# Pools that lie over released ones: waits tile by tile instead of for the whole pool, in a two-layer graph network on one core

## The chip, the core and the metric

The kernel runs on one core of a Trainium2 chip. Its engines are named as the profile names them: PE (matrix products), DVE, ACT and POOL (element-wise work; POOL also issues indirect transfers), and SP, which only issues transfers. Each engine works through its own instructions in order. The metric is the device time of one execution in microseconds (us), as the median of several runs.

## The reference: what is computed

The input is 64 graphs of 256 nodes with 256 features (16384 rows in all) and an integer adjacency. Two layers, each with a graph part and a feed-forward part, all with a residual and a layer norm ahead:

```python
x = x + attention(norm(x), adj, W, a)            # layer 0, graph: softmax over neighbours
x = x + mamba2(norm(x), W_in, conv_w, ..., b_lin) # layer 0, feed-forward: a scan over each graph
x = x + relational(norm(x), adj, weight, bias)   # layer 1, graph
x = x + moe(norm(x), gate_w, gate_b, w1, b1, w2, b2)  # layer 1, feed-forward
```

The last one matters here. Each row is given to the one of 8 experts with the highest gate value, at most 2560 rows to an expert:

```python
idx = argmax(softmax(x @ gate_w + gate_b)); pos = running count of rows of that expert
buf[idx, pos] = x                                  # rows beyond the capacity are dropped
hmid = relu(buf @ w1[e] + b1[e]);  ybuf = hmid @ w2[e] + b2[e]
y = ybuf[idx, pos] * probability * kept
```

## The kernel before: two passes, and the memory they share

**Preparation.** `first_pass` opens a pool `wts` for what lasts through pass 1 and, inside it, the pools `prep` and `prep_ps` (L514 on), in which weights are folded together. The last product there is a transpose of the expert biases b1 (L588); DVE copies it out (L590) and SP writes it to a DRAM tensor `b1d` (L591). Then `prep` and `prep_ps` are released, and their bytes in SBUF and their PSUM banks become free for others.

**Pass 1** works on 32 groups of two graphs (512 rows). Its tiles come from one pool, `fast_pool`, and eight PSUM banks, `fast_ps`; both lie over the released `prep` pools. `clear_slots` fills a DRAM table `slots` with a far value through a tile `blank` (L615 on POOL, L616 a transfer on ACT's queue). For each group SP loads x (L803) and adj (L805); PE transposes x (L781) and so on through attention, scan and relational part. At the end of each pair of groups `choose` picks the experts, and POOL scatters one 4-number record for each row into `slots` (L1282). The order in which all five engines receive their instructions in pass 1 is written out by a planner (`Plan`) from fixed costs and due times (PACE, DUE, LATE); it is the same before and after the change.

When all rows are chosen, `list_blocks` makes on DVE the lists of work for pass 2 (L635 to L647, into the tile `work`). Beside this the plan runs two blocks of 512 rows of the expert part early, in the bytes of pass 1's own tiles (`first_block`: products L744 and L1388, row arithmetic on DVE L1394, L420 to L424, L1402 and on ACT L1396, and an indirect scatter of the finished rows to the output, L427 on POOL). The `y` tiles of these blocks have four buffers, so a later row tile is written over an earlier one whose scatter must have landed.

**Pass 2** (`second_pass`) does the rest of the expert part. Its pools `et`, `es` and `eps` lie over pass 1's released ones. A block is 128, 256 or 512 rows of one expert: kinds "quarters", "halves" and "wholes". Ahead of the loops stands a prologue for all three kinds, in this order: slot fetches of blocks 0 and 1 of each kind (SP, L1502, six transfers, each after reading the list with L1494); index copies and gathers of their rows (POOL, L405, L406, L409: 14 gathers of 128 rows, 2 + 4 + 8); the first weights of each kind (SP, w1 L1511, b1 L1514, w2 L1517, b2 L1520; w1 and w2 are 1 MB each); row norm (DVE L415), transposes (PE L1545) and their copies (ACT L1548) of block 0 of each kind. Then, under nested conditions on the counted number of blocks (L1593, L1619), the quarters run, then the halves, then the wholes. A block i asks for the weights of i+1 and the slots and rows of i+2, computes its hidden layer (PE L1563, ACT L1567) and its output (PE L1573, DVE L1578, ACT L1579, DVE row arithmetic), and scatters (L427). Weights have two buffers, slots and rows three. SP and POOL take all this in the order of the program.

A second version of both passes ("slow", for adjacency values that the fast one does not cover) stands behind a condition and does not run with these inputs.

Of the kernel before, what the change touches and what calls it, by code (L numbers as in the profile page):

```python
# [16 lines left out]
PSUM = bass.MemoryType.PSUM  # L17
# [270 lines left out]
def gnn_mamba_rgcn_moe(ctx: ExitStack, tc: tile.TileContext, a: dict, out: bass.AP):  # L288
# [143 lines left out]
    def first_pass(form, pass1):  # L432
# [73 lines left out]
        def relation(pool, banks, dst, r):  # L506

            nc.sync.dma_start(
                out=dst[:, :, 0:D], in_=a["L1_gnn_weight"][r].rearrange("(k p) o -> p k o", p=P)
            )  # L510
            centred(pool, banks, dst[:, :, 0:D], dst[:, :, 0:D], D)
            projected(pool, banks, dst[:, :, D:DG], dst[:, :, 0:D], E + 1)

        with tc.tile_pool(name="prep" + form, bufs=1) as prep, tc.tile_pool(  # L514
            name="prep_ps" + form, bufs=2, space=PSUM
# [96 lines left out]
        def clear_slots(pool):  # L612

            blank = pool.tile([P, E * CAPP * 4 // P], F32, tag="wh", name="blank", bufs=1)
            nc.gpsimd.memset(blank, FAR)  # L615
            nc.scalar.dma_start(out=slots.rearrange("(p j) w -> p (j w)", p=P), in_=blank)  # L616
            nc.vector.memset(seen, 0.0)
# [33 lines left out]
        def list_first(s):  # L651


            v = nc.vector
            tot, full, ends, gap = (s.tile(n + "_", [P, E]) for n in ("tot", "full", "ends", "gap"))
            we, wb, past = (s.tile(n + "_", [P, NEARLY]) for n in ("we", "wb", "past"))
            counted(s, tot)

            def filled():
                v.tensor_scalar(full(), tot(), 512.0, None, ALU.is_ge)  # L660
                for i in range(2, NB + 1):
                    v.scalar_tensor_tensor(full(), tot(), 512.0 * i, full(), ALU.is_ge, ALU.add)

            s.step(DVE, 0.5, filled, [tot], [full])

            def ended():
                v.tensor_copy(ends(), full())
                summed_up(ends())

            s.step(DVE, 0.8, ended, [full], [ends])  # L670

            def took():
                v.tensor_scalar(tot(), ends(), float(NEARLY), None, ALU.min)
                v.tensor_copy(taken[:, 0:1], tot()[:, 0:1])
                v.tensor_sub(taken[:, 1:], tot()[:, 1:], tot()[:, : E - 1])
                v.tensor_scalar(gap(), full(), -1.0, float(NB), ALU.mult, ALU.add)
                v.tensor_copy(wb(), num[:, :NEARLY])

            s.step(DVE, 0.5, took, [ends, full], [tot, gap, wb, s.fixed(taken)])
            walk(s, we, wb, past, NEARLY, ends, gap, NBLK, early)  # L680
# [726 lines left out]
        def group(s, g, js, pair, toks, full=False):  # L1407


            s.of(g)  # L1410
            xe, hide, entries = attention(s, g, js, full)
            ahead = scan(s, g, xe)
            adjT = mix(s, xe, entries, full, *ahead)
            relate(s, js, 4 * (g % 2), full, xe, adjT, pair)
            if g % 2:
                s.of(g + 1, first=False)
                choose(s, toks, pair)
# [3 lines left out]
            mybir.EngineType.Pool, mybir.EngineType.SP,  # L1421
        }
        if form == "fast":
            pool = pass1.enter_context(tc.tile_pool(name="fast_pool", bufs=1))
            banks = pass1.enter_context(tc.tile_pool(name="fast_ps", bufs=1, space=PSUM))
            clear_slots(pool)
            plan = Plan(pool, banks)

            GEARLY = NG - 4
            rows_early = plan.fixed(x3d)  # L1430
            for g in range(NG):
                if g % 2 == 0:
                    pair = {"stored": [rows_early] if g < GEARLY else []}
                group(plan, g, slice(4 * g, 4 * g + 4), pair, tok[:, 4 * (g - 1) : 4 * (g + 1)])
                if g == GEARLY - 1:
                    plan.after(NG)
                    list_first(plan)
            plan.after(NG)
            list_blocks(plan)
            for b in range(NEARLY):  # L1440
                first_block(plan, b, rows_early, x3d[0 : GEARLY * 4 * P])
            with tc.manual_schedule(engines=ENGINES):
                plan.record()
        else:
            pool = pass1.enter_context(tc.tile_pool(name="slow", bufs=1))
            banks = pass1.enter_context(tc.tile_pool(name="slow_ps", bufs=1, space=PSUM))
            clear_slots(pool)
            every = pool.tile([P, R, 2, DG], F32, name="every")
            nc.vector.tensor_copy(every[:, 0], wrel[:, 0])
            for r in range(1, R):  # L1450
                relation(pool, banks, every[:, r], r)
            toks = pool.tile([P, 8], F32, name="toks")
            nc.vector.tensor_copy(toks, tok[:, 0:8])
            with tc.For_i(0, NG // 2, 1) as i:
                pair, at_once = {"wrel": every, "stored": []}, AtOnce(pool, banks)
                for o in range(2):
                    group(at_once, o, bass.ds(8 * i + 4 * o, 4), pair, toks, full=True)
                nc.vector.tensor_scalar(toks, toks, float(8 * P), None, ALU.add)
            nc.vector.memset(taken, 0.0)
            list_blocks(AtOnce(pool, banks))  # L1460


    def second_pass(form, pass2):
        et = pass2.enter_context(tc.tile_pool(name="et" + form, bufs=2))
        es = pass2.enter_context(tc.tile_pool(name="es" + form, bufs=4))
        eps = pass2.enter_context(tc.tile_pool(name="eps" + form, bufs=8, space=PSUM))

        class Blocks:

# [155 lines left out]
    for form in ("fast", "slow"):  # L1625
        with ExitStack() as here:
            if form == "slow":
                again = nc.values_load(
                    general[0:1, 0:1], min_val=0, max_val=P,
                    skip_runtime_bounds_check_because="a count of partitions",  # L1630
                )
                here.enter_context(tc.If(again > 0))
            with ExitStack() as pass1:
                first_pass(form, pass1)
            with ExitStack() as pass2:
                second_pass(form, pass2)
# [34 lines left out]
```

## Time and profile before

| | |
|---|---|
| median of three runs | 2527.34 us (2525.23 to 2528.05) |
| the profiled execution: its own time | 2531.42 us |
| its span, first to last instruction | 2529.7 us |
| mean granted PE clock | 0.974 |
| PE busy | 2366.6 us, 94% of the span |
| DVE, ACT, POOL busy | 76%, 65%, 33% |
| pass 1's first load of adjacency issued | 45.39 us |
| last scatter of pass 1 issued on POOL | 1901.10 us |
| first slot fetch of pass 2 issued | 1904.15 us |
| first product of pass 2's first block | 1927.69 us |

Times inside the execution are counted from the span's first instruction. A row of a timeline gives start, length, engine, line, operation, the written operand before the arrow and the read ones after it, and in brackets how long the engine had been idle and what released it. In the slices of the page each digit is a busy share in tenths over one fortieth of the span. The chain of waits follows the work that ended last back from its end, each step to what released it. The DMA share is the busy share of the core's 16 DMA engines; values slightly over 1 occur in short stretches.

### The profile page before, as it was taken

Reading aid. Unit: us, or ns where it says so; the run is one execution under the profiler, and the core shown is the slowest. Engines: PE = TensorE matmul, PEld = TensorE weight load, DVE = VectorE, ACT = ScalarE, POOL = GpSimd, SP = SyncE. Lnnn points to the kernel's source line nnn. Section 1 sums busy time; section 2 is a strip of 40 time slices with the busy share of each in tenths; the row PEclk is TensorE's granted clock in tenths of the full one; section 3 lists DMA queues with packets and bytes.
Section 4 is the critical chain, followed back from the end, with each engine's and each line's share of the span. In section 5 each row is a group of like instructions: output and inputs, shape, how many; then the busy total and the mean of one; then the engine's idle time right before and its main releaser. Section 6 shows DMA issues by size and latency. Waiting matters only on the chain.

```text
span 2529.7 us, 35024 instructions
## 1 busy us (share of the span) xinstructions
PE 2366.6 (94%) x11451; PEld 1652.4 (65%) x11451; DVE 1918.0 (76%) x4825; ACT 1641.0 (65%) x3720; POOL 826.1 (33%) x762
## 2 busy tenths in 40 slices
PE   5899999999999999999999999999884899999996
PEld 4567766667667666766766676676654666666664
DVE  3899999999989899999999999999762243344433
ACT  1878888878888787888888888787522223232331
POOL 1122424333342433334343333432523222222231
PEclk8999999999999999999999999999997999999998
DMA  3212222322222232222232222222417433333332
GB/s 113 45 22 57 58 63 62 77 56 53 62 54 70 60 75 54 54 62 64 61 76 57 53 62 53 70 58 44 134 34 264 139 119 116 122 112 108 127 112 64
DMA packets 173527, 198.93 MB, mean 79 GB/s; under 512 B 25448, under 2 KB 157870, under 8 KB 173312
## 3 DMA queue, kind: packets, MB, share of 16 engines
q1 hardware_dynamic: 124816, 135.70, 16.6%
q0 software_dynamic: 46816, 58.88, 12.6%
q8 instruction: 98, 1.61, 0.3%
q10 hardware_dynamic: 1680, 1.79, 0.2%
q14 instruction: 117, 0.96, 0.1%
HBM read 112.47 MB, written 45.45 MB: 62 GB/s over the span
## 4 chain that ended last, share of the span: by engine, by line
DVE 32%; issue 30%; PE 16%; POOL 10%; ACT 8%; DMA 3%; POOLq 0%; SPq 0%; ACTq 0%; DVEq 0%
PE ps L744 11%; DVE y L963 8%; POOL rs L752 4%; POOL xg L409 3%; POOL out_dram L427 3%; DVE gate L946 3%; DVE gate L1108 2%; DVE xh L1105 2%; DMA xg<-x3d,place 2%; DVE st L760 2%; DVE dm L1088 2%; PE ps L1095 1%; DVE ev L857 1%; DVE bm L973 1%; DVE ev L859 1%
## 5 line engine op out<-in xcount | busy, mean ns | idle before, releaser
L744 PE MATMUL ps<-xnT,win 128*128 128x512 f32 x1152 | 542.0, 600 | 4.0 <-ACT xnT L786 4.0
L963 DVE SCALAR_TENSOR_TENSOR y<-ps,cw,y 128x510 f32<-128x510 f32 (+2 forms) x480 | 351.5, 739 | 5.1 <-ACT y L956 3.9
L1030 ACT ACTIVATE dm<-ps,cs 128x256 f32<-128x256 f32 (+1 forms) x1024 | 334.4, 477 | 23.4 <-PE ps L744 22.6
L752 POOL TENSOR_TENSOR rs<-ve,mhalf 128x4 f32<-128x4 f32 x96 | 157.8, 1644 | 562.7 <-DVE ve L750 439.3
L744 PEld LDWEIGHTS ps<-xnT,win 128*128 128x128 f32 x1152 | 204.6, 190 | 170.8 <-issue 157.0
L1563 PE MATMUL ps<-xnT,w 128*128 128x512 f32 (+2 forms) x736 | 280.7, 542 | 13.7 <-DMA w<-in_L_ffn_w_dram 6.9
L1573 PE MATMUL ps<-w,hid 128*128 128x256 f32 x1248 | 276.3, 379 | 0.0
L1573 PEld LDWEIGHTS ps<-w,hid 128*128 128x128 f32 x1248 | 235.3, 190 | 38.7 <-issue 8.6
L744 PE MATMUL ps<-wf,gate 128*128 128x265 f32 x1024 | 252.1, 388 | 0.0
L1563 PEld LDWEIGHTS ps<-xnT,w 128*128 128x128 f32 x736 | 135.7, 200 | 148.4 <-issue 140.6
L1088 DVE TENSOR_TENSOR dm<-dm,bc 128x1536 f32<-128x1536 f32 x128 | 225.8, 1766 | 2.3 <-ACT dm L1036 1.0
L1567 ACT ACTIVATE hid<-ps,b 128x512 f32<-128x512 f32 (+2 forms) x184 | 114.5, 623 | 169.1 <-PE ps L1563 166.7
L744 PEld LDWEIGHTS ps<-wf,gate 128*128 128x128 f32 x1024 | 191.6, 190 | 47.9 <-issue 11.2
L1578 DVE TENSOR_TENSOR yv<-ps,b 128x256 f32<-128x256 f32 x78 | 33.1, 425 | 230.5 <-PE ps L1573 230.5
L1095 PE MATMUL ps<-dm,xdt 128*64 128x256 f32 x1024 | 170.5, 399 | 33.7 <-DVE dm L1088 33.2
L1036 ACT ACTIVATE dm<-dm 128x1536 f32<-128x1536 f32 x128 | 198.6, 1554 | 0.0
L1282 POOL DMA_INDIRECT slots<-meta,sl x128 | 128.0, 1000 | 198.2 <-DVE sl L1279 147.6
L427 POOL DMA_INDIRECT out_dram<-yf,place x78 | 77.9, 999 | 314.1 <-DVE yf L1586 312.9
L760 DVE BATCH_NORM_STATS2 st<-x 128x6 f32<-128x256 f32 x384 | 152.1, 415 | 6.9 <-DMA x<-in_x_dram 6.3
L969 ACT ACTIVATE xh<-y 128x512 f32<-128x512 f32 x160 | 101.2, 632 | 75.5 <-DVE y L963 65.1
L744 PE MATMUL ps<-wh,eT 128*128 128x273 f32 x512 | 142.6, 407 | 7.5 <-ACT eT L882 4.8
L1579 ACT ACTIVATE yv<-yv,meta 128x256 f32<-128x256 f32 x78 | 39.8, 510 | 168.0 <-DVE yv L1578 168.0
(314 smaller groups left out, 5032.4 us busy)
## 6 DMA issues: line engine op xcount, KB each, us to landing
w<-in_L_ffn_w_dram SPq DMA_DIRECT2D x52, 1024.0 KB
x<-blin POOLq DMA_DIRECT2D x32, 530.0 KB
x<-brel POOLq DMA_DIRECT2D x32, 530.0 KB
adji<-in_adj_dram SPq DMA_DIRECT2D x32, 512.0 KB
x<-in_x_dram SPq DMA_DIRECT2D x32, 512.0 KB
x3d<-x SPq DMA_DIRECT2D x32, 512.0 KB
out_dram<-x SPq DMA_DIRECT2D x32, 512.0 KB
cm<-bm SPq DMA_DIRECT2D x32, 128.0 KB
```

The source lines that it names most:

```text
L427: apart("out", nc.gpsimd.indirect_dma_start(out=outf, out_offset=bass.IndirectOffsetOnAxis(ap=col, axis=0), in_=yf, in_offset=None, bounds ...
L744: nc.tensor.matmul(out_, lhsT=lhsT, rhs=rhs, start=(i == 0), stop=(i == len(pairs) - 1))
L752: s.step(POOL, 1.0, lambda: nc.gpsimd.tensor_tensor(rs(), ve(), mhalf[:, 0:4], ALU.pow), [ve], [rs])
L760: s.step(DVE, 0.34, lambda j=j: nc.vector.bn_stats(sb()[:, j, :], src()[:, j, 0:D]), [(src, j)], [(sb, j)])
L963: nc.vector.scalar_tensor_tensor(y3[:, :, d:], p3[:, :, : N - d], cw[:, c, k : k + 1], y3[:, :, d:], ALU.mult, ALU.add,)
L1030: nc.scalar.activation(dm()[:, q, bi, o : o + n], ps()[:, t0 + N - n : t0 + N], AF.Relu, bias=cs()[:, j, h : h + 1], scale=-1.0,)
L1036: s.step(ACT, 1.38, lambda: nc.scalar.activation(dm(), dm(), AF.Exp, scale=-1.0), [], [dm])
L1088: s.step(DVE, 1.67, lambda dm=dm: nc.vector.tensor_mul(dm(), dm(), bc().unsqueeze(1).to_broadcast([P, 2, 2, N + P])), [bc], [dm])
L1095: nc.tensor.matmul(o, lhsT=xdt()[:, 2 * bi, h * 64 : (h + 1) * 64], rhs=dm()[:, q, bi, 0:N], start=True, stop=False,)
L1282: s.step(POOL, 1.1, lambda j=j: apart("slots", nc.gpsimd.indirect_dma_start(out=slots, out_offset=bass.IndirectOffsetOnAxis(ap=sl()[:, j : ...
L1563: nc.tensor.matmul(ps[:, :n], lhsT=w1[:, k, f * P : (f + 1) * P], rhs=xnT[:, k, :], start=(k == 0), stop=(k == 1),)
L1573: nc.tensor.matmul(ps[:, :D], lhsT=hid[:, f, j * P : (j + 1) * P], rhs=w2[:, f, :], start=(f == 0), stop=(f == NFT - 1),)
```

## The change

A tile pool that is opened over bytes of a released pool must not write them before their former users are done. Before, the first user of a new pool on each engine waits for everything that the released pools' tiles were last used for, and later users need not ask again. With `reuse_waits="tile"` each tile of the new pool waits at its own first use, only for those who used the bytes that it lies on. The same is asked for all seven pools of this kind:

```diff
         if form == "fast":
-            pool = pass1.enter_context(tc.tile_pool(name="fast_pool", bufs=1))
-            banks = pass1.enter_context(tc.tile_pool(name="fast_ps", bufs=1, space=PSUM))
+            pool = pass1.enter_context(tc.tile_pool(name="fast_pool", reuse_waits="tile", bufs=1))
+            banks = pass1.enter_context(tc.tile_pool(name="fast_ps", reuse_waits="tile", bufs=1, space=PSUM))
...
-            pool = pass1.enter_context(tc.tile_pool(name="slow", bufs=1))
-            banks = pass1.enter_context(tc.tile_pool(name="slow_ps", bufs=1, space=PSUM))
+            pool = pass1.enter_context(tc.tile_pool(name="slow", reuse_waits="tile", bufs=1))
+            banks = pass1.enter_context(tc.tile_pool(name="slow_ps", reuse_waits="tile", bufs=1, space=PSUM))
...
-        et = pass2.enter_context(tc.tile_pool(name="et" + form, bufs=2))
-        es = pass2.enter_context(tc.tile_pool(name="es" + form, bufs=4))
-        eps = pass2.enter_context(tc.tile_pool(name="eps" + form, bufs=8, space=PSUM))
+        et = pass2.enter_context(tc.tile_pool(name="et" + form, reuse_waits="tile", bufs=2))
+        es = pass2.enter_context(tc.tile_pool(name="es" + form, reuse_waits="tile", bufs=4))
+        eps = pass2.enter_context(tc.tile_pool(name="eps" + form, reuse_waits="tile", bufs=8, space=PSUM))
```

In the built program the instructions of every engine, their order and the addresses of all tiles are the same as before. The waits that differ, in the fast form, with what each stands for:

| instruction | waits before | waits after |
|---|---|---|
| POOL L615, fill of `blank` | all of `prep`'s users, b1d's landing among them | loads of two weights, a DVE copy L497 and a PE product L500 of the preparation |
| ACT L616, `blank` to `slots` | the same | the fill alone |
| SP L805, first adjacency | the same | the loads of the norm weight and of the attention vector |
| SP L803, first x | nothing more (it stands behind L805) | the load of W_out and a PE transpose of it, L572 |
| PE L781, first transpose | all of `prep`'s loads and x | x, and the DVE copy L590 |
| SP L1502, first slot fetch of pass 2 | all last users of pass 1's pools, the eight L427 of the second early block's and first early block's rows among them | the list (L647), the last L1282, a PE product L744 |
| SP L1502, the other five | nothing more | a PE product L1388, an ACT copy L1379 of the first early block |
| POOL L405, first index copy | all last users of pass 1 | its slot fetch, a weight load of an early block, a PE product |
| POOL L409, gathers | the index copy | the index copy, pass 1's stores of x, and the earlier indirect transfer on the same of eight semaphores (L427's for the first eight) |
| SP L1511, w1 of the first quarter | nothing more | a PE product L744 of the second early block |
| SP L1517, w2 of the first half | nothing more | loads and a DVE operation of groups 30 and 31 |
| SP L1511, w1 of the first whole | nothing more | the last four L427 of pass 1, and the last ACT L1396 |
| SP L1517, w2 of the first whole | nothing more | the four L427 before those |
| DVE L1612, first of pass 2 | all last users of pass 1 | nothing |

## The prediction

> **What bounds the kernel now.** I read the core's span, then the page's slices, then the queue's own waits on SP, the chain of waits around the joint of the two passes, and the timelines of PE and SP there. The slices say where there is anything to win:
>
> ```profile
> span 2529.7 us, 35024 instructions
> ...
> PE   5899999999999999999999999999884899999996
> ...
> PEclk8999999999999999999999999999997999999998
> DMA  3212222322222232222232222222417433333332
> ```
>
> A slice is 63 us. PE is at 9 almost throughout; pass 1 and the whole blocks of pass 2 stand on it, and no wait at a pool's first use can help there. The low digits are the first slice (the head of pass 1) and slices 29 to 31, the joint, where DMA jumps to 7. SP's own waits name what holds the joint:
>
> ```profile
> SPq L1502 <- DMA out_dram<-y,hide: 30.8, 2, 28.4
> ```
>
> SP has its first slot fetch of pass 2 (L1502) in hand when the block lists are written (L647, 1872.1) and then sits until pass 1's last row scatter has landed. The chain of waits shows the last of it:
>
> ```profile
> 1900.39 0.44 DVE y L1402
> 1900.83 0.27 issue
> 1901.10 2.43 DMA out_dram<-y,hide
> ...
> 1904.15 1.60 DMA meta<-slots
> ...
> 1906.35 0.19 POOL place L405
> ```
>
> So all loading for pass 2 begins at 1904.15: six slot fetches until 1908.7, then weights (SP: first at 1909.20), all while PE has been idle since 1895.0. What it costs PE is in its timeline (start, length, line, operands, in brackets the idle time before):
>
> ```profile
> 1911.47 0.66 PE L1545 MATMUL ps<-ident,xn 128*128 128x128 f32 x2 [16.43 <-DVE xn L415]
> ...
> 1927.69 5.71 PE L1563 MATMUL ps<-xnT,w 128*128 128x128 f32 x32 [0.16 <-issue]
> ...
> 1940.15 3.81 PE L1563 MATMUL ps<-xnT,w 128*128 128x128 f32 x32 [3.08 <-DMA w<-in_L_ffn_w_dram]
> ...
> 1951.23 5.47 PE L1563 MATMUL ps<-xnT,w 128*128 128x128 f32 x32 [0.30 <-ACT xnT L1548]
> ...
> 1960.67 3.84 PE L1563 MATMUL ps<-xnT,w 128*128 128x128 f32 x32 [0.30 <-ACT xnT L1548]
> ```
>
> The four long rows are quarter blocks q0 to q3. The head of pass 1 has the same shape, smaller:
>
> ```profile
> 43.09 0.39 SPq L591 DMA_DIRECT2D b1d<-b1t  x1
> 45.39 0.38 SPq L805 DMA_DIRECT2D adji<-in_adj_dram  x1
> 45.81 3.95 SPq L803 DMA_DIRECT2D x<-in_x_dram  x5
> 51.95 1.94 PE L781 MATMUL ps<-ident,x 128*128 128x128 f32 x8 [9.35 <-DMA x<-in_x_dram]
> ```
>
> **The change, part by part.** [...]
>
> *Head.* Before, the first adjacency load waits for the landing of b1d (issued 43.09, released 45.25). After, it waits for two loads issued before 10, and x tile 0 for a PE transpose over by 36.6, so they follow b1d in SP's queue: the first at 43.09 + 0.39 + about 0.05 = 43.5 instead of 45.39, 1.85 us. The fill of slots (320 KB, issued 46.14 among the x loads) moves to about 35.5, when its memset's new waits are over. At the 378 GB/s of these loads it took up to 0.85 us of their time; x tile 0 is issued ahead of it and shares only partly, so I take 0.35 and keep 0 and 0.85. b1d's 32 KB now run beside the loads: they took 2.16 us alone and are mostly latency; 0 to 0.4 back, within the same span. Head: **-2.2** (-1.5 to -2.7). It reaches the end: everything up to the joint is queued behind x tile 0 in a fixed order, and PE's busy share is 98% from 104 us on.
>
> *Joint, SP.* The first slot fetch now waits for pass 1's last slot scatter (issued 1868.64) and for PE work over by 1872; the list ends it at 1872.3. With the old spacing (1904.15 to 1909.20) the weights of the first quarter and first half start at about 1877.5, 4.4 MB; at the 371 GB/s of the row 1928 to 1937 they are in by about 1890, instead of 1924. Behind them on SP stands the first whole block's w1, whose tile lies on bytes that pass 1's last scatters read: it still waits for 1903.5. It then goes at 1904.1 instead of 1923.66, and the second quarter's weights at about 1908 to 1912 instead of 1931.6. Nothing else is queued behind that wait, and 13 us of slack stand before it.
>
> *Joint, POOL.* POOL is in order, so its index copies (L405) come after its last scatter, which occupies it until 1902.07; with a 0.3 us step, 1902.35 instead of 1906.35: 4.0 us. Its 14 gathers run back to back (1907.15 to 1926.7), so all move by 4.0.
>
> *Joint, PE.* PE reaches q0 after the whole block's last transpose, 1.36 us after the last of its gathers is normed (1926.33). That gather was issued at 1920.15, so it took 6.2 us among weights, where the first one, ahead of them, took 3.6 (1907.15 to 1910.74). After: issued at 1916.1. The Trainium skill (DMA: Bandwidth & Descriptors, Queues, rings and completion order) says that a DMA engine goes round robin between queue rows packet by packet, so that a gather should not stand behind SP's whole backlog; then 3.6 us hold, and q0 starts at 1921.1, 6.6 us early. The row speaks against it: 6.2 (8.0 for the first half's gather) with two weight sets in flight, and after the change two sets are in flight again (first whole, second quarter, from 1904.1); by the row q0 starts at 1923.7, 4.0 early. By bytes: 4.3 MB of weights and 1.3 MB of gathers at 371 GB/s are through at 1919.2, and one gather's 1 to 2 us puts the norm at 1920.2 to 1921.2, q0 at about 1922. I take **-5.0**.
>
> q1 waited 3.08 us for weights; they now land by about 1920, q0 ends at 1931.9. A gap of 0.3 (q3's) is left: **-2.8**. q2 waited 3.08 us for its row norm, that is a gather issued at 1943.97 behind a slot fetch that took 5.9 us (1937.59 to 1943.48). That fetch is now made long before; the gather follows q0's output at about 1934.1 and has until 1939.1, 5.0 us, with about 1 MB beside it instead of 3 to 4: **-3.1**, or 0.9 us of stall left if it takes the old 5.9. q2's first layer took 5.47 against 3.84 us for q3, at a granted clock of 0.57 in 1952 to 1956. The skill (TensorE: Matmul & The Clock Gate, Part 1) has the clock drop after one idle window of about 3.4 us that runs free; the rows fit only half, as the equal gap before q1 left the clock at 1.00. Either way a gap of 0.3 before q3 kept it: **-1.6**, or 0 if a stall stays. q0 stays cold, as PE idles over 12 us before it. From q3 on I change nothing: the gaps of 3.82 and 6.01 us where the quarter and half loops are left have the branch (L1619) beside them, and the whole blocks are PE's.
>
> Joint: -5.0 - 2.8 - 3.1 - 1.6 = -12.5. The added waits on SP, ACT and POOL are semaphore instructions of 17 to 43 ns on events long past; a dozen costs under 0.5 us, beside idle time.
>
> *Sum.* -2.2 - 12.5 = **-14.7**. The profiled execution took 2531.4 us (span 2529.7 and 1.7 around it) and would take 2516.7. It lies 4.1 above the median of the three runs, 2527.34; against that, 2512.6.
>
> **Rivals.**
>
> *Only the queue moves.* Transfers pace q1 and q2 anyway (DMA share 1.03 to 1.09 in every 4 us from 1924 to 1952), the stalls come back behind other loads, and only POOL's 4.0 and the head's 2.2 are left: 2521.1. For it: the saturated rows. Against: the bytes are fewer in that window, as 4.4 MB have moved to before 1890, where the DMA share was 0.09 to 0.17.
>
> *Gathers pass the weights*, as the round-robin rule has it, and the first half block and the branch exits speed up a little on emptier queues: -6.6 in place of -5.0, and a microsecond or two more: 2509.5.
>
> *It does not do what it says.* Some tile of the prologue still lies over the last scatter's source and its wait holds the queue for the rest. The built program shows such a wait only at the first whole block's w1, behind everything early. If PE's start were still fixed by that set, only the head would be left: 2525.1, no change by measure.
>
> *Slower: the early weights delay pass 1's own scatters.* Pass 1's last two blocks write their rows through four y buffers, and a buffer is rewritten by DVE or ACT only when its scatter has landed. Now 4.4 MB run at 1877.5 to 1890 beside the scatters issued at 1878.36, 1880.95 and 1883.35. A scatter took 2.43 us on a quiet queue; the rewrites come 6.5 to 8.1 us after the issues (1883.35 to 1890.25; 1892.41 to 1898.94). At 8.0 us, the worst loaded row, this costs 1.1 to 1.5 us, part of it under DVE's 2.94 us of idle before 1895.07. Beyond 6.5 each microsecond is one on the path; all of the gain is gone at about 21 us, and only from there is the kernel slower; at 28 us it would be 2534. Against it: no row near that. DVE's row work (L423, 0.42) has the same length at DMA share 1.08 as at 0.1.
>
> **How the numbers follow.** The sum, 2512.6: 0.55. Only the queue, 2521.1: 0.22. Gathers pass, 2509.5: 0.08. Nothing but the head, 2525.1: 0.10. Slower, 2534: 0.05. A measurement of this kernel tells about 0.2%, 5 us, from no change; "only the queue" lies near that edge and gives 0.02 to it: faster 0.83, same 0.12, slower 0.05. The range takes the sum's own bounds (-10 to -20: gather lags, q2's stall and clock, the head) and nearly all of the second case: 2506 to 2522.
>
> **What would show it.** Right: the first adjacency load at 43.5, PE's L781 near 49.8; slot fetches at about 1870 (1872 less the head's gain) and weights from about 1875; POOL's L405 about 0.3 us after the last L427; q0's L1563 some 21.6 us after that last L427 starts instead of 26.6 (1901.10 to 1927.69), and q1, q2 and q3 without gaps above 0.3 and 3.8 long. Wrong: a weight stall before q1 or a cold q2 (then the second case), or DVE's L421 and L1394 of the last two blocks waiting for out_dram (then the last).

## The result and the profile after

Five runs of the changed kernel gave a median of 2511.73 us (2511.02 to 2516.22), five of the kernel before beside them 2528.05 (2525.23 to 2532.42): a ratio of 0.9939 (0.9925 to 0.9954), 15.4 us less (11.6 to 19.0). Forecast were 2512.6 us, 14.7 less. The profiled execution took 2511.58 us, its span is 2509.9.

```profile
span 2509.9 us, 35018 instructions
...
PE   5999999999999999999999999999986899999996
...
PEclk8999999999999999999999999999997999999998
DMA  3212222322222322222232222223337433333332
```

PE has risen in slice 2, just behind the head, and in slices 29 and 31, the joint (8 to 9, 8 to 9, 4 to 6); in slices 28 to 31 the DMA digits are 3337 instead of 2417: loading begins earlier. SP's own waits (sum, number, longest) no longer have L1502 waiting for `out_dram`. The wait has moved to the first whole block's w1, as foreseen:

```profile
SPq L1511 <- DMA out_dram<-y,hide: 13.5, 2, 11.1
```

SP's timeline of the joint shows what had gone ahead of it: six slot fetches from 1868.24, the first weights from 1873.46, and, once the weights of the first quarter and first half are all asked for at 1884.15, nothing until the held w1 at 1898.29:

```profile
1868.24 4.66 SPq L1502 DMA_DIRECT2D meta<-slots  x6
1873.46 0.38 SPq L1511 DMA_DIRECT2D w<-in_L_ffn_w_dram  x1
...
1878.09 6.06 SPq L1520 DMA_DIRECT2D b<-in_L_ffn_b_dram  x1
1898.29 0.38 SPq L1511 DMA_DIRECT2D w<-in_L_ffn_w_dram  x1
```

In the table by stretches, the DMA share from 1878 to 1890, under pass 1's last products, is 0.92 where it was 0.10. POOL goes straight from its last scatter to the index copies and gathers:

```profile
1895.67 0.97 POOL L427 DMA_INDIRECT out_dram<-y,hide  x1 [1.43 <-DVE other L1612]
1896.64 0.21 POOL L405 CAST place<-meta 128x1 int32<-128x1 f32 x1
1897.37 1.07 POOL L409 DMA_INDIRECT xg<-x3d,place  x1 [0.28 <-POOL place L406]
```

and PE's first four blocks follow each other; the waits for weights and for the row norm are gone. The third block is warm: its 32 products take 3.84 us at a granted clock of 1.00, where before they took 5.47 at 0.57. (Below, a quarter block whose 32 products take 3.8 us is called warm, one in which they take 5 us or more cold.)

```profile
1904.12 0.69 PE L1545 MATMUL ps<-ident,xn 128*128 128x128 f32 x2 [14.51 <-DVE xn L415]
...
1917.98 5.73 PE L1563 MATMUL ps<-xnT,w 128*128 128x128 f32 x32 [0.16 <-issue]
...
1927.64 3.84 PE L1563 MATMUL ps<-xnT,w 128*128 128x128 f32 x32 [0.25 <-ACT xnT L1548]
...
1935.66 3.84 PE L1563 MATMUL ps<-xnT,w 128*128 128x128 f32 x32 [0.30 <-ACT xnT L1548]
...
1943.47 3.84 PE L1563 MATMUL ps<-xnT,w 128*128 128x128 f32 x32 [0.30 <-ACT xnT L1548]
```

The head, from the timelines of SP and PE: the adjacency load is 0.48 us behind b1d's store instead of 2.30.

```profile
40.90 0.39 SPq L591 DMA_DIRECT2D b1d<-b1t  x1
41.38 0.53 SPq L805 DMA_DIRECT2D adji<-in_adj_dram  x1
42.01 4.33 SPq L803 DMA_DIRECT2D x<-in_x_dram  x5
47.89 1.94 PE L781 MATMUL ps<-ident,x 128*128 128x128 f32 x8 [7.48 <-DMA x<-in_x_dram]
```

The two profiles' spans differ by 19.8 us, more than the timed runs. 2.19 us of that lie ahead of every changed wait (b1d's store at 40.90 instead of 43.09; in twelve further profiles 41.88 to 43.15), 0.80 in pass 1's last 62 products (L1388, 15.25 instead of 16.05 us), 1.69 in the first half block's hidden layer (7.14 instead of 8.83). These 4.7 us are in work that the change leaves as it is. So stretches are compared below, each from a fixed event to another, over several profiles.

### The profile page after: what moved, and what is told of

It is laid out like the page before. It is cut to its first block, busy times and chain, and to the rows that moved or that the text cites. A ratio compares the mean times of both kernels' runs of the same rounds, so it can differ in the third digit from the quotient of the medians.

```text
span 2509.9 us, 35018 instructions
## 1 busy us (share of the span) xinstructions
PE 2360.5 (94%) x11451; PEld 1645.5 (66%) x11451; DVE 1917.8 (76%) x4825; ACT 1644.8 (66%) x3720; POOL 817.3 (33%) x762
## 4 chain that ended last, share of the span: by engine, by line
issue 31%; DVE 30%; PE 18%; POOL 10%; ACT 7%; DMA 3%; POOLq 0%; another core or an unknown queue 0%; SPq 0%; ACTq 0%; DVEq 0%
PE ps L744 12%; DVE y L963 8%; POOL xg L409 3%; POOL out_dram L427 3%; DVE gate L946 3%; POOL rs L752 3%; PE ps L1095 2%; DVE gate L1108 2%; DVE st L760 2%; DVE xh L1105 2%; DVE dm L1088 2%; DMA xg<-x3d,place 1%; DVE ev L857 1%; DVE bm L973 1%; DVE ev L859 1%
## 5 line engine op out<-in xcount | busy, mean ns | idle before, releaser
L744 PE MATMUL ps<-xnT,win 128*128 128x512 f32 x1152 | 544.5, 602 | 4.0 <-ACT xnT L786 4.0
L752 POOL TENSOR_TENSOR rs<-ve,mhalf 128x4 f32<-128x4 f32 x96 | 149.0, 1552 | 570.3 <-DVE ve L750 447.6
L744 PEld LDWEIGHTS ps<-xnT,win 128*128 128x128 f32 x1152 | 205.4, 191 | 171.8 <-issue 156.9
L744 PE MATMUL ps<-wf,gate 128*128 128x265 f32 x1024 | 251.9, 388 | 0.6 <-DVE gate L1108 0.6
L1088 DVE TENSOR_TENSOR dm<-dm,bc 128x1536 f32<-128x1536 f32 x128 | 225.9, 1766 | 2.8 <-ACT dm L1036 1.4
L744 PEld LDWEIGHTS ps<-wf,gate 128*128 128x128 f32 x1024 | 191.3, 190 | 48.6 <-issue 11.2
L1095 PE MATMUL ps<-dm,xdt 128*64 128x256 f32 x1024 | 170.4, 399 | 32.8 <-DVE dm L1088 32.3
L1282 POOL DMA_INDIRECT slots<-meta,sl x128 | 127.9, 1000 | 200.5 <-DVE sl L1279 149.3
L427 POOL DMA_INDIRECT out_dram<-yf,place x78 | 77.8, 997 | 310.9 <-DVE yf L1586 310.2
L744 PE MATMUL ps<-wh,eT 128*128 128x273 f32 x512 | 142.4, 407 | 7.4 <-ACT eT L882 4.9
```

Of the source, the lines that this page charges most:

```text
L427: apart("out", nc.gpsimd.indirect_dma_start(out=outf, out_offset=bass.IndirectOffsetOnAxis(ap=col, axis=0), in_=yf, in_offset=None, bounds ...
L744: nc.tensor.matmul(out_, lhsT=lhsT, rhs=rhs, start=(i == 0), stop=(i == len(pairs) - 1))
L752: s.step(POOL, 1.0, lambda: nc.gpsimd.tensor_tensor(rs(), ve(), mhalf[:, 0:4], ALU.pow), [ve], [rs])
L1088: s.step(DVE, 1.67, lambda dm=dm: nc.vector.tensor_mul(dm(), dm(), bc().unsqueeze(1).to_broadcast([P, 2, 2, N + P])), [bc], [dm])
L1095: nc.tensor.matmul(o, lhsT=xdt()[:, 2 * bi, h * 64 : (h + 1) * 64], rhs=dm()[:, q, bi, 0:N], start=True, stop=False,)
L1282: s.step(POOL, 1.1, lambda j=j: apart("slots", nc.gpsimd.indirect_dma_start(out=slots, out_offset=bass.IndirectOffsetOnAxis(ap=sl()[:, j : ...
```

## The experiments

The experiments ran on four chips, on which the kernel before took 2485.16, 2483.97, 2545.43 and 2529.26 us; only ratios to it, and stretches within a profile, are set side by side. All compute the same; what they change is waits and the order of requests. In the table all times count from the start of pass 1's last scatter (POOL L427, 1901.10 before and 1895.67 after): POOL's first index copy L405, the first layers of the quarter blocks q0 to q3, and the span's end.

| kernel | L405 | q0 | q1 | q2 | q3 | end | timed ratio |
|---|---|---|---|---|---|---|---|
| before | 5.25 | 26.59 | 39.05 | 50.13 | 59.57 | 628.60 | 1 |
| before again | 5.24 | 26.74 | 39.11 | 49.74 | 57.55 | 628.58 | |
| head alone | 5.25 | 26.88 | 39.14 | 50.22 | 59.66 | 628.51 | 0.9989 |
| changed | 0.97 | 22.31 | 31.97 | 39.99 | 47.80 | 614.23 | 0.9939 |
| changed, again | 0.97 | 22.77 | 32.65 | 40.92 | 48.73 | 619.61 | 0.9952 |
| changed, beside | 0.97 | 22.53 | 32.01 | 40.09 | 47.91 | 617.99 | 0.9943 |
| joint alone | 0.95 | 22.31 | 31.90 | 40.23 | 48.04 | 615.29 | 0.9947 |
| weights late | 0.97 | 23.24 | 35.41 | 46.18 | 53.99 | 624.16 | 0.9982 |
| slots late | 4.81 | 26.10 | 36.15 | 44.76 | 52.57 | 622.18 | 0.9969 |
| turned later | 0.97 | 9.15 | 21.03 | 33.53 | 42.72 | 615.37 | 0.9950 |
| q1's weights early | 0.97 | 20.13 | 28.84 | 36.65 | 44.47 | 613.47 | 0.9938 |
| q1's weights early, beside | 0.96 | 20.67 | 30.09 | 37.91 | 45.72 | 616.33 | 0.9945 |
| both | 0.97 | 9.16 | 18.27 | 30.71 | 41.01 | 611.82 | 0.9931 |
| both, beside | 0.97 | 9.30 | 24.39 | 34.94 | 42.75 | 616.10 | 0.9945 |

The theory: two separate places, the head and the joint, and in the joint both POOL's and SP's requests count. The rivals: only the queue of slots and gathers moves; or something else beside these places.

**The joint alone**: the changed waits only for pass 2's three pools.

```diff
-pool = ...(tc.tile_pool(name="fast_pool", reuse_waits="tile", bufs=1))
-banks = ...(tc.tile_pool(name="fast_ps", reuse_waits="tile", bufs=1, space=PSUM))
+pool = ...(tc.tile_pool(name="fast_pool", bufs=1))
+banks = ...(tc.tile_pool(name="fast_ps", bufs=1, space=PSUM))
```

> Only the three pools of pass 2 wait tile by tile; pass 1's pools wait as before. My theory (head 1.9 us, joint 4.3 of queue + 2.8 + 3.1 + 1.6): 11.8 us faster than before, first adjacency load still about 2.3 us after b1d, q1 to q3 without gaps over 0.3. Rival, that the head is worth the 4.1 us by which PE's first transpose moved in the changed kernel's profile: 11.3 or less here and 4.1 in the head-only kernel.

0.9947 (0.9934 to 0.9961), 13.2 us less, where 11.8 was expected. The rival's 11.3 or less lies inside the interval too (9.7 to 16.4). Its PE rows in the joint are those of the changed kernel, and its adjacency load is 2.29 us behind b1d's store, as before:

```profile
1877.42 5.67 PE L1563 MATMUL ps<-xnT,w 128*128 128x128 f32 x32 [0.16 <-issue]
...
1887.01 3.84 PE L1563 MATMUL ps<-xnT,w 128*128 128x128 f32 x32 [0.24 <-ACT xnT L1548]
...
1895.34 3.84 PE L1563 MATMUL ps<-xnT,w 128*128 128x128 f32 x32 [0.30 <-ACT xnT L1548]
```

**The head alone**: the reverse, the new waits for pass 1's two pools only.

```diff
-et = ...(tc.tile_pool(name="et" + form, reuse_waits="tile", bufs=2))
+et = ...(tc.tile_pool(name="et" + form, bufs=2))
```

and so for `es` and `eps`.

> Only pass 1's two pools wait tile by tile. My theory: 1.9 us faster, the first adjacency load 0.5 us after b1d instead of 2.3, and the joint as before, with gaps of about 3 us ahead of q1 and q2. Rival (the profile's 4.1 us at PE's first transpose is all the change's): 4.1 us faster. Rival (pass 1 swallows it later): 0.

0.9989 (0.9982 to 0.9995), 2.7 us less (1.2 to 4.5), where 1.9 was expected. Of the rivals, 0 is outside the interval and 4.1 just inside; against 4.1 stands the stretch from b1d's store to PE's first transpose, 2.4 us shorter on the mean of all profiles (below). SP's timeline has the adjacency load 0.49 us behind b1d's store; the joint is that of before to 0.3 us, PE's waits for weights and the cold third block included:

```profile
1880.97 5.74 PE L1563 MATMUL ps<-xnT,w 128*128 128x128 f32 x32 [0.15 <-issue]
...
1893.23 3.81 PE L1563 MATMUL ps<-xnT,w 128*128 128x128 f32 x32 [2.85 <-DMA w<-in_L_ffn_w_dram]
...
1904.31 5.46 PE L1563 MATMUL ps<-xnT,w 128*128 128x128 f32 x32 [0.30 <-ACT xnT L1548]
```

13.2 + 2.7 = 15.9 beside the 15.4 of the first comparison: the two places add up, within the intervals.

**The weights late**: slots and gathers are left to wait tile by tile, but the weight and bias tiles are in a pool of their own that waits for everything.

```diff
+ew = pass2.enter_context(tc.tile_pool(name="ew" + form, bufs=2))
...
-getattr(self, name).append(et.tile(
+home = ew if name in ("w1", "w2", "b1", "b2") else et
+getattr(self, name).append(home.tile(
```

> The changed kernel, but the weight tiles of pass 2 stand in a pool of their own that waits for all of pass 1, so slot fetches are early and weights are not. My theory, in which queue, weights and slot fetch each carry a part: POOL's index copy still right after its last scatter, q0's weights only after that scatter has landed, a gap of about 2 us back ahead of q1 and about 3 ahead of q2; 7.4 us faster than before. Rival, the weights were hidden and POOL's start is everything: 13.6 faster, no gaps. Rival, the weights are everything: 1.9 faster.

0.9982 (0.9974 to 0.9991), 4.5 us less (2.2 to 6.5), where 7.4 was expected: a miss, outside the interval. Its line numbers in pass 2 are two higher than those of before (and so in the next kernel). SP's timeline shows the weights held, but only three of the six slot fetches early, at 1825.39 to 1827.5. The other three, presumably because the added pool puts the tiles of `et` on other bytes, wait for a DVE operation (L424) and a row scatter, until 1852:

```profile
1825.39 28.71 SPq L1504 DMA_DIRECT2D meta<-slots  x6
1855.33 0.38 SPq L1513 DMA_DIRECT2D w<-in_L_ffn_w_dram  x1
...
SPq L1504 <- DMA out_dram<-y,hide: 16.1, 1, 16.1
```

That held nothing up: POOL's copies and gathers run without a gap behind its last scatter, and the weights were held longer still. PE shows the weight stall of before, with a cold second block behind it:

```profile
1875.88 5.21 PE L1565 MATMUL ps<-xnT,w 128*128 128x128 f32 x32 [0.90 <-ACT xnT L1550]
...
1888.05 5.44 PE L1565 MATMUL ps<-xnT,w 128*128 128x128 f32 x32 [3.30 <-DMA w<-in_L_ffn_w_dram]
```

POOL's 0.97 is all there, q0 is 3.35 early, and from q1 on the stalls of before eat into it. The joint gained 5.58 by q3 (59.57 to 53.99), where 5.5 was expected, and 4.4 by the end: the half block then waited 4.53 us for its b1 (before, 3.82 for a weight) and its hidden layer took 9.37 (8.83). With 2.5 in the head (from b1d's store to L781, 6.41 beside 8.93) that makes 6.9 us in the profile; why the timed runs gave 4.5 stays open. "Only the queue moves" describes this kernel, not the changed one.

**The slots late**: the weights of the first quarter and first half go ahead, slot tiles wait for everything.

```diff
+em = pass2.enter_context(tc.tile_pool(name="em" + form, bufs=2))
...
+home = em if name == "meta" else et
...
+for blocks in three[:2]:
+    blocks.fetch_weights(0)
 for blocks in three:
     for i in range(2):
         blocks.fetch_slots(i)
...
-for blocks in three:
-    blocks.fetch_weights(0)
+wholes.fetch_weights(0)
```

> The changed kernel, but the slot tiles of pass 2 stand in a pool that waits for all of pass 1, and the first quarter's and first half's weights are asked for ahead of the slots: weights early, POOL late. My theory: POOL's index copy about 5 us after its last scatter starts (as before), q0 26 us after it, but no gaps ahead of q1 and q2 and a warm q2: 9.4 us faster than before. Rival, POOL's start is everything: 1.9 faster. Rival, the weights are everything: 13.6 faster.

0.9969 (0.9957 to 0.9981), 7.7 us less (4.7 to 10.7), where 9.4 was expected; both rivals, 1.9 and 13.6, are outside. POOL waits for its slots as before, and yet q1 starts 0.25 us after what it needs, with no weight stall. The timeline of POOL, then of PE:

```profile
1854.32 0.97 POOL L427 DMA_INDIRECT out_dram<-y,hide  x1 [1.43 <-DVE other L1615]
1859.13 0.19 POOL L405 CAST place<-meta 128x1 int32<-128x1 f32 x1 [3.84 <-DMA meta<-slots]
```

```profile
1890.47 3.84 PE L1565 MATMUL ps<-xnT,w 128*128 128x128 f32 x32 [0.25 <-ACT xnT L1550]
1899.08 3.84 PE L1565 MATMUL ps<-xnT,w 128*128 128x128 f32 x32 [0.30 <-ACT xnT L1550]
```

Each half of the change in the joint gives a part: by q3 5.6 us with the slots alone and 7.0 with the weights alone; both together gave 11.8 (59.57 to 47.80).

**The kernel before, once more**, for a second profile of it.

> The kernel before once more, for a second profile of it. My theory: the parts of the two profiles' difference that I don't ascribe to the change are chance of PE's clock: b1d's issue differs from 43.09 by up to 2 us, the last 62 products of pass 1 take anything from 15.1 to 16.5 us and the first half's L1563 7.1 to 9.4, while the starts of q0, q1, q2, q3 counted from the last scatter of pass 1 stay within 0.5 of 26.6, 39.1, 50.1 and 59.6. Rival, these parts belong to the change too: the second profile repeats 43.1, 16.0 and 8.8 within 0.2.

```profile
1882.06 5.49 PE L1563 MATMUL ps<-xnT,w 128*128 128x128 f32 x32 [0.16 <-issue]
...
1894.43 5.44 PE L1563 MATMUL ps<-xnT,w 128*128 128x128 f32 x32 [3.21 <-DMA w<-in_L_ffn_w_dram]
...
1904.32 0.44 PE L1545 MATMUL ps<-ident,xn 128*128 128x128 f32 x2 [0.99 <-DVE xn L415]
1905.06 3.84 PE L1563 MATMUL ps<-xnT,w 128*128 128x128 f32 x32 [0.30 <-ACT xnT L1548]
```

Two of the chance parts came out as expected (b1d at 42.63, the 62 products 15.74 us); the half's layer, 9.93, went beyond the 7.1 to 9.4 allowed for. None repeats the first profile, so the rival is out. q0 to q2 are within 0.4; q3 is 2.0 earlier, which was not expected. This time the cold block is q1, and the slower q1 gives q2's gather the time it lacked: the stall is 0.99 instead of 3.08. Of the 2 us, 1.5 are given back by the first whole block's first layer (92.56 after the last scatter, 93.09 in the first profile), the rest later: both profiles end 628.6 us after it. Which block turns cold differs from one execution to the next.

**The other blocks turned later**: only the first quarter is normed and transposed ahead of the loops, the half and the whole at the start of theirs, so that q0 does not stand behind 14 gathers.

```diff
-for blocks in three:
-    blocks.turned(blocks.norm(0), 0)
+quarters.turned(quarters.norm(0), 0)
...
 for blocks in three:
+    if blocks is not quarters:
+        blocks.turned(blocks.norm(0), 0)
```

> The changed kernel, with row norm and transposes of the first half and the first whole block moved from the prologue to the start of their loops, so that q0 stands behind its own gather alone. My theory, that after the change q0 is held by the gathers of all three kinds on POOL: q0 starts about 9.5 us after the last scatter of pass 1 instead of 22.3; the half and the whole give 2 to 3 us each back at their own start, q2 perhaps 1: 8 us faster than the changed kernel, 22 faster than before. Rival, q0 is held by weights still on their way: no gain over the changed kernel.

0.9950 (0.9936 to 0.9964), 12.4 us less than before where 22 was expected. q0 came at 9.15, as expected; PE's timeline shows where its 13 us went:

```profile
1861.98 5.44 PE L1563 MATMUL ps<-xnT,w 128*128 128x128 f32 x32
...
1873.86 3.81 PE L1563 MATMUL ps<-xnT,w 128*128 128x128 f32 x32 [2.77 <-DMA w<-in_L_ffn_w_dram]
...
1885.62 0.50 PE L1545 MATMUL ps<-ident,xn 128*128 128x128 f32 x2 [3.92 <-DVE xn L415]
...
1907.08 1.30 PE L1545 MATMUL ps<-ident,xn 128*128 128x128 f32 x4 [4.02 <-DVE xn L415]
...
1932.15 1.94 PE L1545 MATMUL ps<-ident,xn 128*128 128x128 f32 x8 [6.88 <-DVE xn L415]
```

q1 waits for its weights again (they are asked for after the held first whole's). q2 waits for its gather, which POOL issued only at 1879.38: its slot fetch was asked for at 1870.92 (SP) and landed 8.0 us later, as DVE's index copy shows:

```profile
1878.90 0.15 DVE L405 CAST place<-meta 128x1 int32<-128x1 f32 x1 [6.16 <-DMA meta<-slots]
```

And the half and the whole pay for their own norm at the branch where their transposes used to be done. At the first whole's first layer nothing is left: 81.52 after the last scatter, beside 79.35, 82.89 and 81.50 in the three profiles of the changed kernel. What a stretch gains is not what the end gains, when the next stretch waits for the same loads.

**The second quarter's weights ahead of the first whole's**, and then **both** edits.

```diff
-self.fetch_weights(i + 1)
+if self.kind < 2 or i > 0:
+    self.fetch_weights(i + 1)
...
 for blocks in three:
+    if blocks is wholes:
+        quarters.fetch_weights(1)
     blocks.fetch_weights(0)
```

> The changed kernel, with the second quarter's weights asked for ahead of the first whole's, so that 6.6 MB instead of 4.4 run beside the end of pass 1 and 2.2 less beside the gathers. My theory: the gathers' lag of 6.3 us comes from these weights, it falls to about 4 and q0 starts 2 us earlier: 2 us faster than the changed kernel, 15.6 faster than before. Rival, the mechanism by which I would have expected the change to be slower (row buffers of pass 1 held by scatters that lag beside the weights) now reaches the path: DVE waits for out_dram at L421 or L1394 by 2 us or more in the last rows of the second early block, and the last scatter comes that much later; no gain or a loss of 1 to 3 us.

> Both of the last two changes together. My theory: q0 starts about 9 us after pass 1's last scatter, no weight stall before q1; 9 us faster than the changed kernel, 23 faster than before. Rival, the scatters' lag eats it: as in the kernel with only the moved norm and transposes, or 1 to 3 us slower than it.

The first: 0.9938 (0.9925 to 0.9952), 15.4 less, where 15.6 was expected. q0 starts 2.2 us earlier, and the whole block's last gather is normed 4.2 us after its issue, as the theory had it (6.35 in the changed kernel; 4.7 in the later profile of this edit). The rival is there too, smaller: L421 waits 1.18 and 0.39 us for scatters, and from the end of pass 1's last L1388 to the last scatter it is 6.61 us, 6.05 to 6.07 in the profiles without this edit. The table counts from that scatter and doesn't show this half microsecond.

The second: 0.9931 (0.9918 to 0.9945), 17.1 less, where 23 was expected; q1 has lost its weight stall, and the third block waits 4.25 us for its row norm in its place.

**The changed kernel again**, then **it and both variations on one chip**, as the earlier comparisons had put them on different ones.

> The changed kernel once more, on the chip of the experiments, to set it beside its two parts and its two variations. Theory (head and joint are separate terms): the ratios of the joint alone (0.9947) and the head alone (0.9989) multiply to 0.9936, so 0.9936, within 0.0015; adjacency load 0.5 us after b1d's issue, L405 about 1.0 after the last scatter of pass 1, q0 at +22.3, q1 at +31.9 to +32.0, q2 at +40.0 to +40.2, q3 at +47.8 to +48.0. The 19.8 us by which the two profiles first shown differ hold 4.7 us of chance: this profile's span is then 13 to 17 us under that of the kernel before on this chip (2483.9), not 19.8. Rival (the profiles' 19.8 us are the change, and the timed ratio is low by chance): span 2464 and ratio near 0.992. Variations: if asking for the second quarter's weights ahead of the first whole's is worth nothing, this run is within 0.001 of 0.9938; if it is worth the 1 to 2 us that q0 came earlier there, this run is near 0.9945.

0.9952 (0.9938 to 0.9966), 12.2 us less. The ratio is 0.0016 above the product of the two parts, just outside what was expected, and q0 to q3 are 0.5 to 0.9 later than in the first profile of this kernel. This run was on a third chip, where the kernel before took 2545.43 us, so the span of 2483.9 named in the expectation can't be its measure, and it decides nothing about the variations.

> The changed kernel beside the two variations below, all three on one chip with the same runs of the kernel before: the earlier runs put them on different chips, so their ratios (0.9952 for this one, 0.9938 and 0.9931) can't be set against each other. Theory (head and joint as separate terms, 13.6 us by the stretches of the two profiles first shown): ratio 0.9946, within 0.001. Rival (the first timed ratio, 0.9939, is the truth and there is something beside the two places): 0.9939 or under, with a last scatter of pass 1 that comes earlier by over 4 us than head and chance explain.

> The changed kernel with the first half's and whole's norm and transposes moved to their loops and the second quarter's weights asked for ahead of the first whole's. Theory A (both variations gain a little: the stall before the second quarter is gone, the rest of what the first quarter gains is given back at the half's and whole's own starts): 4 to 7 us under the changed kernel of this call, ratio near 0.9925. Rival (all is given back, the earlier 0.9931 was the chip): within 2 us of the changed kernel of this call.

> The changed kernel with only the second quarter's weights asked for ahead of the first whole's. Theory A (the whole block's gathers and the norms come 2 us earlier, as fewer bytes lie beside them): 1 to 3 us under the changed kernel of this call. Rival (no difference): within 1 us of it; the ratio is then near 0.9946.

Beside each other: the changed kernel 0.9943 (0.9930 to 0.9956), both edits 0.9945 (0.9932 to 0.9957), the early weights alone 0.9945 (0.9924 to 0.9966). The changed kernel is where the theory had it (0.9946, within 0.001), and no variation beats it by measure. For both edits that settles it: 4 to 7 us were expected, and the medians are 1.0 apart (2514.22 and 2515.23). For the early weights alone it stays open: 1 to 3 us were expected, q3 starts 2.2 us earlier than in the changed kernel beside it and the end comes 1.7 earlier after the last scatter, and the timed interval is 10 us wide. In the run of both edits the second block waited 5.80 us for an ACT copy that waited 6.84 for something the profile does not name, which the earlier run of the same kernel did not show.

## Why the prediction was right, point by point

*The sum.* Three comparisons of the changed kernel gave 15.4, 12.2 and 14.4 us less, 14.0 on the mean. By stretches it is the same: from b1d's store to PE's first transpose 2.4 us (below), from the last scatter to the end 11.8 (628.56 on the mean of the three profiles with the old joint, 616.78 on that of the four with the new one): 14.2 beside the forecast 14.7, 2.2 for the head and 12.5 for the joint. Some of that closeness is luck. By q3, up to which the forecast's terms reach, the same profiles have gained 10.8 of the 12.5 (58.93 to 48.12); the last 1.0 comes behind q3, where single profiles of one joint differ by up to 4.5 us.

*Head: right.* From b1d's store to the adjacency load 2.29 to 2.30 us with the old waits and 0.48 to 0.49 with the new: 1.81, where 1.85 was put. From there to L781, the fill of `slots` in or out of the way, the first pair of profiles showed only 0.05 (6.56 to 6.51), but three profiles with the old waits have 6.56 to 6.77, mean 6.64, and eleven with the new 5.75 to 6.51, mean 6.04: 0.6, between the bounds 0 and 0.85, above the 0.35 taken. That it passes through pass 1 is seen at the last scatter: from b1d's store to it, on one chip 1813.23 us in the profile with the old waits and 1811.24 on the mean of three with the new, on another 1812.69 and 1810.71. (PE was 98% busy in the 100 us from 104 on; up to 1800 it is 97%.)

*Joint, POOL: right.* L405 from 5.25 to 0.97 after the last scatter: 4.28, put at 4.0. It starts at the scatter's own end, without the 0.3 us step that was allowed for.

*Joint, q0: 5.0 was too much, 4.3 is what came* (26.74 on the mean of three profiles, 22.48 on that of four). This is the term of the sum that was mis-sized: POOL's 4.0 came, the up to 1 us on top, from faster gathers, did not. From L405 to q0 it took 21.34 us in the first profiles before and after alike. The working had a row (6.2 us for a gather among weights), a rule (queues served in turn, so 3.6) and an estimate by bytes, and took a value in between; the row alone was right. The gather that q0 waits for is the whole block's last, issued at 1910.32 on POOL and normed 6.35 us later on DVE, where the row had 6.2:

```profile
1910.32 0.95 POOL L409 DMA_INDIRECT xg<-x3d,place  x1 [0.30 <-issue]
...
1916.67 0.41 DVE L415 TENSOR_SCALAR xn<-xg,meta 128x256 f32<-128x256 f32 x1 [0.53 <-DMA xg<-x3d,place]
```

The first gather of pass 2, which before went ahead of all weights, shows the load most plainly. DVE's first row norm, before and after:

```profile
1910.74 0.41 DVE L415 TENSOR_SCALAR xn<-xg,meta 128x256 f32<-128x256 f32 x1 [6.54 <-DMA xg<-x3d,place]
...
1903.66 0.41 DVE L415 TENSOR_SCALAR xn<-xg,meta 128x256 f32<-128x256 f32 x1 [7.95 <-DMA w<-in_L_ffn_w_dram]
```

Before, its gather was issued at 1907.15: 3.6 us. After, at 1897.37: 6.3 us. (The second row puts the wait down to a weight load; the norm reads only xg and meta, and in the two later profiles of the changed kernel the row names xg, with 6.4 us.) With the slots late, where this gather again ran ahead of weights, it took 3.66. That a DMA engine goes round in turn between queue rows, as the Trainium skill has it (DMA: Bandwidth & Descriptors, Queues, rings and completion order), is not refuted by this; that a gather therefore keeps its quiet time is. "Gathers pass the weights" did not happen.

*q1, q2 and the clock: right.* q1's stall gone, 2.80 (put at 2.8); q2's gone, 3.06 (3.1); q2 warm, 1.63 (1.6). These three are from one pair of profiles. In the second profile of before the cold block was q1 and the stalls were other ones, but their sum came back mostly by the first whole block. So the total is firmer than its terms; on the means of the three and four profiles the three steps are 2.7, 2.8 and 1.1. What turns a block cold was only half understood in the prediction: by the rows ahead of q1, gaps of 2.77, 2.85 and 3.08 us left it at 3.81, gaps of 3.21 and 3.30 at 5.44, so a limit of the gap's length may lie between; but q2, with 3.08 ahead of its transposes, took 5.47. The Trainium skill (TensorE: Matmul & The Clock Gate, Part 1) has the clock drop after one idle window of about 3.4 us that runs free. Taken at its word, none of these gaps fills such a window and no block should have turned cold; those at 3.21 and 3.30, and q2's, did. These runs do not settle what does it. Gaps of 0.2 to 0.3 left q1 to q3 of the changed kernel at 3.84 in all three of its profiles.

*The rival that was slower: its mechanism is there, its price is not.* Early weights do hold back pass 1's scatters. DVE's timeline of the changed kernel:

```profile
1886.69 0.29 DVE L421 TENSOR_SCALAR y<-y 128x256 f32<-128x256 f32 x1 [1.78 <-DMA out_dram<-y,hide]
...
1889.65 0.42 DVE L1394 TENSOR_TENSOR y<-ps,hide 128x256 f32<-128x256 f32 x1 [1.07 <-issue]
```

The scatter it waited for was issued at 1878.73, 7.96 us earlier, nearly the worst loaded row (8.0) from which 1.1 to 1.5 us were worked out, partly under idle time. (The shortest time from issue to rewrite before was 6.34 us, 1890.00 to 1896.34, not 6.5.) Here all of the delay was under idle time: the next L1394 needs PE's last L1388, which ends at 1889.61, and DVE was idle 1.07 us before it. From the end of that L1388 to the last scatter it is 6.06 us, and 6.07 before. A later profile of the same kernel shows two such waits, 0.35 and 0.89, and 6.05. It costs nothing here because the next row tile had to wait for PE longer still, not because the transfers were undisturbed. With a third set of weights early the slack no longer covers it in three of four profiles: 6.42 to 6.61.

*What was left out.* From q3 on nothing was changed in the forecast. From q3 to the end it is 569.03, 571.03 and 568.85 us with the old joint (profiles in the order of the table), and 566.43, 570.88, 570.08 and 567.25 with the new: no difference beyond chance.

## What to carry to other kernels

Read a pool-wide wait by what is queued behind it. Here the wait itself was for 128 rows, but SP's first fetch, and with it six slot loads and 4.4 MB of weights, stood behind it for 28.4 us, and the gain was in the stalls that this caused three blocks later, more than in the wait. When a transfer is estimated beside others, take the row of the trace in which the same transfer ran beside the same load, not an average with a rule. And test the parts alone before adding an improvement on top: moving q0 up by 13 us gained nothing at the end.

## What the runs showed of the hardware

- An indirect gather of 128 rows of 1 KB was normed 3.6 us after its issue where it ran ahead of the weight loads (four profiles), and 6.2 to 8.4 us after it beside weight loads and other gathers; with one set of weights fewer beside it the whole block's last one took 4.2 and 4.7 in two profiles. A row scatter landed after 2.43 us on a quiet queue and after 7.96 beside weight loads.
- The same kernel took 2484 to 2545 us on the chips of these runs. Instructions are equally long where this was compared (the 1152 products of L744 600 ns on the mean on one chip, 601 on another), but PE is busy for 482.5 of the 500 us from 500 to 1000 on the first chip, and for 496.4 on one of the quick ones. In that stretch PE's L1095 waits five times for DVE's L1088, 10.8 to 12.0 us together, in four profiles from the slower chips, and not at all in two from the quick ones; why DVE is late there stays open.
- Profiles of one kernel differ. The two of the kernel before are 2.0 us apart at q3 and 0.02 at the end (from the last scatter), the three of the changed kernel, on three chips, 0.9 at q3, 3.5 at the first whole's first layer and 5.4 at the end. A difference of two profiles' spans (19.8 here) was a worse measure of the change (14) than stretches taken over several.
